# A Mamba and attention kernel on one core: three exps ahead, three work banks, and an input added by a transfer

## The chip, the core and the metric

The kernel runs on one core of one Trainium2 chip. The core has engines that run side by side, each through its own queue of instructions in order: PE (TensorE, matrix products into PSUM), DVE (VectorE), ACT (ScalarE), POOL (GpSimd) and SP (SyncE, which here only issues DMA transfers). The metric is the device time of one execution in microseconds (us), the median of the runs. Time before: 8270.61 us, median of 3 runs (8264.9 to 8275.63).

## The reference, cut to what matters

The input x has 4 images of 512 channels and 64 x 64 positions, in float32. Two layers are added to it, each on its group norm:

```python
# layer 0: group norm, layer norm over the channels, then 4 chunks of 128 channels through one Mamba
x = x + mamba_block(_gn(x))
# inside, for each chunk: in_proj, a causal convolution of 4 taps, silu, then for each position
h = exp(dt * A) * h + (dt * xc) * B        # 256 inner channels x 16 states
y = (h * C).sum(over states)
# y + xc * D, times silu(z), out_proj, plus skip * chunk; layer norm; a projection 512 -> 512
# layer 1: linear attention with 8 heads on the group norm of the result
x = x + attention(_gn(x))                  # q, k relu; kq = k^T q over all positions; out_proj
```

The recurrence over the 4096 positions of an image is what takes most of the time. The group norm of layer 1 needs the statistics of the whole image after layer 0, so an image's attention starts when its last tile has left layer 0.

## The kernel before, in words

**Steps and slots.** A tile is 512 positions of one image. A step is one tile and one chunk of 128 channels: 4 images x 8 tiles x 4 chunks = 128 steps, numbered n, with c the chunk. A step has 16 slots (SLOTS), and each slot s is one function call, `slot`. In it DVE runs two scans of 128 x 512 (L602: h = dA * h + bx along the positions), which need an exp dA from ACT (L576, `decay`) and a product bx from POOL (L584, `drive`, issued two slots ahead). `decay` writes dA into PSUM, in a pool of LEAD banks; the exp for scan k + LEAD is put in ACT's queue behind scan k, and can start when scan k has read its bank. Then DVE multiplies the states of one slot by C (L625, `product`), mostly between the two scans of the next slot; in slots 3 and 11 the slot's own product comes at its end as well, and slots 4 and 12 have none. C's rows come from PE, which spreads them to 128 partitions in the one bank c_all (`c_row`), once for two slots: it can be filled when the second product has read it and must be full for the next one. The last quarter of the positions is multiplied by POOL (L613). `fold_states` lets PE sum the states into y.

**The order of the work.** Inside `tc.manual_schedule()` the instructions stand as the Python code issues them. At the end of each slot `after` issues the rest: first what is due, then fixed items by slot number (softplus of the next step's dt in slot 2, with two table loads; the copy `with_skip` in slot 5; silu in slot 10), then pieces of the background work. That work is written as generators in the queues `ahead` (the next tile's norms), `late` (`projected`: the second layer norm, the projection 512 to 512 and the sum with x) and `rest` (the attention of the image before). A budget of matmuls (`credit`) and the number of PSUM banks held (`limit[0]`, asked for by `room`) say how much of it is let in.

**Banks and results.** PSUM has eight banks: y 1, c_all 1, dA LEAD = 2, and four work banks (`ps_w`) that all other matmul groups share. A group's result is taken from its bank by ACT (or DVE). `later(2, what)` issues that copy two slots after the matmuls, so that the engine that takes it does not stand waiting for PE.

**The sum with x** (`projected`, L413 to L443): the tile of x is loaded again by SP into a buffer xr (`load_x`), of which there are three, shared by tag with the attention's tiles. PE adds it to the projection in the bank with four small matmuls at once against a 32 x 32 identity, `fold`; ACT takes the sum and its bias into xr (L421); one slot later DVE takes the group norm's statistics of that quarter (L423, `bn_stats`); SP stores the tile (L442).

**After the slots** the last image's projection and attention run alone, bounded by PE.

Of the kernel before, what the change touches and what calls it, by code (L numbers as in the profile page):

```python
# [14 lines left out]
P = 128  # L15
T = 512
# [8 lines left out]
def kernel(  # L25
# [40 lines left out]
    wk = ctx.enter_context(tc.tile_pool(name="wk", bufs=2))  # L66
    LEAD = 2

# [3 lines left out]
    ps_d = ctx.enter_context(tc.tile_pool(name="ps_d", bufs=LEAD, space=bass.MemoryType.PSUM))  # L72
    ps_w = ctx.enter_context(tc.tile_pool(name="ps_w", bufs=4, space=bass.MemoryType.PSUM))

# [49 lines left out]
    def no_tile(spare=0):  # L124
        return now[0] is not None and held_x[0] + spare >= TILES

    def load_now(src, name):
        held_x[0] += 1
        xt = wk.tile([P, NC, T], F32, tag="x", name=name, bufs=TILES)
        nc.sync.dma_start(xt, src)  # L130
        return xt
# [163 lines left out]
    def stats_end(stats, name):  # L295

        mv = small.tile([P, NC, 2], F32, tag="mv", name=f"mv_{name}")
        for c in range(NC):
            nc.vector.bn_aggr(mv[:, c, :], stats[:, c, :, :].rearrange("p t s -> p (t s)"))
        cm = small.tile([P, NC], F32, tag="cm", name=f"cm_{name}")  # L300
        nc.vector.tensor_copy(cm, mv[:, :, 0])
        pm = work_bank(f"pm_{name}")
        mm(pm[:, 0:NC], grp, cm, start=True, stop=True)
        gm = small.tile([P, NC], F32, tag="gm", name=f"gm_{name}")
        nc.vector.tensor_copy(gm, pm[:, 0:NC])
        dev = small.tile([P, NC], F32, tag="dev", name=f"dev_{name}")
        nc.vector.tensor_tensor(dev, cm, gm, ALU.subtract)
        nc.vector.tensor_tensor(dev, dev, dev, ALU.mult)
        nc.vector.tensor_tensor(dev, dev, mv[:, :, 1], ALU.add)
        pv = work_bank(f"pv_{name}")  # L310
        mm(pv[:, 0:NC], grp, dev, start=True, stop=True)
        gr = small.tile([P, NC], F32, tag="gr", name=f"gr_{name}", bufs=4)
        nc.vector.tensor_scalar(gr, pv[:, 0:NC], 1e-5, None, ALU.add)
        free(2)
# [21 lines left out]
    def layer_norm(v, name, gained):  # L336


        def means(parts, what, when):
            yield from room()  # L340
            sums = work_bank(f"{what}_sums_{name}")
            for c in range(NC):
                mm(
                    sums[c * LANE : (c + 1) * LANE, :], ones, parts[c],
                    start=True, stop=True, abreast=NC,
                )
            got = wk.tile([P, T], F32, tag="sq", name=f"{what}_got_{name}", bufs=4)

            def take():
                nc.scalar.copy(got, sums)  # L350
                free()

            copied = later(2, take)
            yield
            yield from until(copied)
            yield when
            yield from room(when)
            bank = work_bank(f"{what}_{name}")
            mm(bank, mean.to_broadcast([P, P]), got, start=True, stop=True)
            return bank  # L360
# [21 lines left out]

        rooted = later(2, root)
        yield
# [28 lines left out]
    def projected(ym, stats, x1, b, t):  # L413

        nm = f"{b}_{t}"
        yield from layer_norm(ym, f"b_{nm}", False)
        xt = yield from load_x(b, t, "r")
        taken = []

        def take(o, pp):  # L420
            nc.scalar.activation(xt[:, o, :], pp, AF.Identity, bias=pb[:, o : o + 1])  # L421
            free()
            later(1, lambda: nc.vector.bn_stats(stats[:, o, t, :], xt[:, o, :]))  # L423

        for o in range(NC):
            yield from room()
            pp = work_bank(f"pp_{nm}_{o}")
            for c in range(NC):
                mm(
                    pp, w_pr[:, c, o * P : (o + 1) * P], ym[:, c, :],  # L430
                    start=(c == 0), stop=False,
                )
                if c == 1:
                    yield "more"
            for k in range(P // BLK):
                r = slice(k * BLK, (k + 1) * BLK)
                mm(pp[r, :], fold[r, :], xt[r, o, :], abreast=P // BLK, start=False, stop=True)
            taken.append(later(2, lambda o=o, pp=pp: take(o, pp)))
            yield
        yield from until(*taken)  # L440
        yield from pause(1)
        nc.sync.dma_start(x1, xt)  # L442
        later(2, free_x)  # L443


    def inputs(f, xn, c, nm):
# [14 lines left out]
        for e in range(NH):  # L461
            pc[e] = work_bank(f"pc_{nm}_{e}", 0)
            taps(e, range(NTAP // 2))
            yield
            taps(e, range(NTAP // 2, NTAP))
            later(2, lambda e=e: take(e))
            yield
        for e in range(NH):
# [5 lines left out]

            later(2, lambda e=e, pz=pz: nc.scalar.copy(xz[:, 1, e, :], pz))
            yield
# [197 lines left out]
    def attention(b, x1s, stats):  # L674
# [35 lines left out]
        def sums(v):  # L710
# [5 lines left out]
            for p in range(NC):  # L716
                for i in range(P // HEAD):
# [4 lines left out]
                    )  # L722
            return later(2, lambda: add(pk, v == 0))

        fetch(0, "a")
        yield
        norm = stats_end(stats, f"b{b}")
        yield
        for v in range(NT * SUB):
# [5 lines left out]
            for j in range(2):  # L735
# [14 lines left out]
                qk[i] = both[:, 1 + i % 3, :]  # L750
                ready[i] = later(2, lambda i=i, pq=pq: relu(i, pq))
                if u:
# [34 lines left out]
        for p in range(NC):  # L787
            yield from room()
            pm = work_bank(f"pm2_{b}_{p}")
            mm(pm, kqn[:, p, :], m2[:, p, :], start=True, stop=True)  # L790
            taken.append(later(2, lambda p=p, pm=pm: take2(p, pm)))
            yield
# [11 lines left out]
        for m in range(NC):  # L804
            yield from room()
            pm = work_bank(f"pm3_{b}_{m}")
            for p in range(NC):
# [4 lines left out]
                if p == 1:  # L812
                    yield "more"
            taken.append(later(2, lambda m=m, pm=pm: take3(m, pm)))
            yield
# [9 lines left out]
        for o in range(NC):  # L825
# [7 lines left out]
            for m in range(NC):  # L833
# [3 lines left out]
                )  # L837
            taken.append(later(2, lambda o=o, pm=pm: offset(o, pm)))
            yield
# [14 lines left out]
        for t in range(NT):  # L854
            x1 = yield from fetched(t, "b")
            for o in range(NC):
                yield from room()
                pp = work_bank(f"pr_{b}_{t}_{o}")
                for m in range(NC):
# [4 lines left out]
                    if m == 1:  # L864
                        yield "more"
                later(2, lambda t=t, o=o, pp=pp: store(t, o, pp))
                fetch(t + 1, "b")
# [21 lines left out]
    def input_norm(b):  # L889
        stats = stats_tile(f"st0_{b}")  # L890
        yield from stats0(stats, b)
        norms[b] = stats_end(stats, f"a{b}")
        yield
# [71 lines left out]
    with tc.manual_schedule():  # L965
        credit, seen, mix, held[0], held_x[0] = 0.0, work["mm"], iter(()), 0, 0
        for n, (b, t, c) in enumerate(steps):
# [10 lines left out]
            for s in range(SLOTS):  # L978
                def after():
# [17 lines left out]
                    if s == 2 and nxt is not None:  # L997
                        nc.scalar.preload_act_table_set("softplus")
                        time_steps(nxt, names[n + 1])
                        nc.scalar.preload_act_table_set("natural_log_exp_and_others")  # L1000
                    if s == 5 and before is not None:
                        pb_, pt_, pc_ = steps[n - 1]
# [28 lines left out]

                    limit[0] = 3 if 9 <= s < 13 else 2
                    credit = min(credit + 3.5 - (work["mm"] - seen), 2.6)
# [76 lines left out]
```

## Time and profile before

| | before |
|---|---|
| median of 3 runs | 8270.61 us |
| the profiled execution's own time | 8270.61 us |
| its span | 8268.9 us |
| busy: PE | 6698.2 us (81%) |
| busy: DVE | 7187.9 us (87%) |
| busy: ACT | 5366.3 us (65%) |
| busy: POOL | 6856.1 us (83%) |
| first scan, last scan begin | 122.5 us, 7805.7 us |

A row of a group has the line, the engine and the operation, what it writes and reads, how often; then the busy time of all, the mean of one in ns, and the idle time of the engine just before them with what ended it. A wait has who waited, for whom, the total in us, the number and the longest. A row of the timeline has its start, its length, and in brackets the idle time before it.

### The profile page before, as it was taken

To read this page: it belongs to the slowest core of one execution; us is meant where nothing else is said; L and a number is where in the kernel's file an instruction comes from. 1 tells how busy PE (TensorE), PEld (TensorE's weight loads), DVE (VectorE), ACT (ScalarE), POOL (GpSimd) and SP (SyncE) were. 2 spreads that over 40 slices of the span, in tenths; PEclk is the share of its full clock that TensorE was granted. 3 is DMA by queue.
4 is the path that set the end of the run, shared out by engine and by line. 5 is a ranking of instruction groups with operands and counts; after the bars stand their busy time and mean duration, and the time that the engine had idled before them with its cause. 6 is when DMAs were issued, how large, how long until landed. Compare 5 with 4: busy or idle time off the path is not lost. (4 is left out here: it accounts for less than half of the span.)

```text
span 8268.9 us, 89639 instructions
## 1 busy us (share of the span) xinstructions
PE 6698.2 (81%) x23450; PEld 2248.1 (27%) x23520; DVE 7187.9 (87%) x6890; ACT 5366.3 (65%) x7841; POOL 6856.1 (83%) x4565
## 2 busy tenths in 40 slices
PE   5677777767788888888788888888788888888699
PEld 1122222112222222322222222232223223233244
DVE  5999999999999999988999999988889999998700
ACT  4666666666666776666677766667667666666421
POOL 4999899999888888888888988888889888888600
PEclk8788888778899989999899999899889999989799
DMA  5666665666666666666666666566666655666412
GB/s 159 165 162 160 146 152 144 155 148 159 164 162 151 155 161 151 161 177 169 165 153 161 164 160 160 149 161 179 161 154 157 156 144 148 152 175 180 120 39 87
DMA packets 829317, 1266.32 MB, mean 153 GB/s; under 512 B 183920, under 2 KB 317568, under 8 KB 816512
## 3 DMA queue, kind: packets, MB, share of 16 engines
q1 hardware_dynamic: 821632, 1255.87, 60.3%
q10 hardware_dynamic: 7168, 4.71, 0.2%
q8 instruction: 184, 3.01, 0.2%
q14 instruction: 333, 2.73, 0.1%
HBM read 1053.28 MB, written 206.57 MB: 152 GB/s over the span
## 5 line engine op out<-in xcount | busy, mean ns | idle before, releaser
L584 POOL TENSOR_TENSOR bx<-d_all,b_all 128x1024 f32<-128x1024 f32 x2048 | 4793.8, 2360 | 98.7 <-DVE h L602 82.1
L602 DVE TENSOR_TENSOR_SCAN h<-dA,st,bx 128x512 f32<-128x512 f32 x3584 | 4432.6, 1269 | 236.4 <-ACT dA L576 141.8
L576 ACT ACTIVATE dA<-d_all,a_t 128x512 f32<-128x512 f32 x4096 | 2803.6, 689 | 2227.3 <-DVE h L602 2202.4
L625 DVE TENSOR_TENSOR h<-h,c_all 128x768 f32<-128x768 f32 x2048 | 1909.2, 932 | 256.0 <-PE c_all L120 246.1
L613 POOL TENSOR_TENSOR h<-h,c_sb 128x512 f32<-128x512 f32 x1024 | 1298.2, 1268 | 110.4 <-DMA c_sb<-c_rows 18.3
L120 PE MATMUL y<-h,fold 128*32 128x512 f32 x8192 | 1278.2, 700 | 122.7 <-POOL h L613 118.7
L120 PE MATMUL c_all<-parts,sel 128*128 128x384 bf16 x1024 | 374.2, 365 | 1097.2 <-DVE h L625 1094.7
L120 PE MATMUL pq<-w_qk,xa 128*128 128x512 f32 x2048 | 1039.8, 640 | 10.7 <-issue 5.1
L120 PE MATMUL pc<-xn,w_cv 128*128 128x512 f32 x2048 | 1015.5, 626 | 39.9 <-ACT res L850 15.6
L612 POOL COPY st<-h 128x4 f32<-128x4 f32 x1024 | 192.7, 188 | 631.1 <-DVE h L602 583.5
L602 DVE TENSOR_TENSOR_SCAN h<-dA,bx 128x512 f32<-128x512 f32 x512 | 602.7, 1209 | 93.3 <-ACT dA L576 84.4
L120 PEld LDWEIGHTS <-sel 128*128 128x128 bf16 x1280 | 127.7, 100 | 1864.8 <-DVE h L625 1632.3
L120 PEld LDWEIGHTS pc<-xn,w_cv 128*128 128x128 f32 x2048 | 377.8, 197 | 698.9 <-issue 564.0
L120 PEld LDWEIGHTS pq<-w_qk,xa 128*128 128x128 f32 x2048 | 411.4, 205 | 496.2 <-issue 472.9
L120 PE MATMUL pr<-xb,m 128*128 128x512 f32 x1024 | 514.5, 641 | 7.9 <-ACT parts L531 5.9
L120 PE MATMUL pp<-xn,w_pr 128*128 128x512 f32 x1024 | 516.3, 630 | 3.8 <-DVE xn L387 3.8
L120 PE MATMUL pt<-dt,w_dt 32*128 32x512 f32 x512 | 270.7, 885 | 108.1 <-ACT parts L531 55.0
L120 PEld LDWEIGHTS y<-h,fold 128*32 128x32 f32 x8192 | 171.0, 114 | 665.9 <-issue 343.9
L120 PE MATMUL y<-xz,dg 128*128 128x512 f32 x512 | 344.6, 763 | 0.0
L649 POOL TENSOR_TENSOR xz<-xz 128x512 f32<-128x512 f32 x256 | 325.2, 1270 | 2.7 <-ACT xz L646 2.7
L494 POOL TENSOR_TENSOR dt<-dt,xz 128x1024 f32<-128x1024 f32 x128 | 302.6, 2364 | 20.7 <-DMA c_rows<-dt 20.7
L120 PE MATMUL pd<-xz,w_xp 128*128 128x512 f32 x512 | 293.1, 702 | 7.8 <-ACT xz L919 7.8
(156 smaller groups left out, 6141.9 us busy)
## 6 DMA issues: line engine op xcount, KB each, us to landing
d_all<-d_rows SPq DMA_DIRECT2D x2048, 256.0 KB, 6.6
b_all<-b_rows SPq DMA_DIRECT2D x4096, 64.0 KB, 2.2
d_rows<-dt SPq DMA_DIRECT2D x256, 512.0 KB, 2.8
c_sb<-c_rows SPq DMA_DIRECT2D x4096, 16.0 KB, 1.8
xs<-in_x_dram SPq DMA_DIRECT2D x32, 1024.0 KB, 6.8
xn<-in_x_dram SPq DMA_DIRECT2D x32, 1024.0 KB, 6.1
xr<-in_x_dram SPq DMA_DIRECT2D x32, 1024.0 KB, 6.1
x<-xr SPq DMA_DIRECT2D x32, 1024.0 KB, 4.3
```

The source lines that it names most:

```text
L120: nc.tensor.matmul(out_, lhsT, rhs, **how)
L494: nc.gpsimd.tensor_tensor(f["both"][:, 1], f["both"][:, 0], f["xz"][:, 0], ALU.mult)
L576: nc.scalar.activation(dAs[k], fs[n]["d_all", e][:, 0, j, :], AF.Exp, scale=a_t[:, e, j, q : q + 1])
L584: nc.gpsimd.tensor_tensor(bxs[g], fs[n]["d_all", e][:, 1, jj * 2 : jj * 2 + 2, :], bc(b_all[g // JJ], 2), ALU.mult)
L602: nc.vector.tensor_tensor_scan(h[:, j, :], dAs.pop(2 * g + i), bxs[g][:, i, :], 0.0 if t == 0 else st[:, c, e, q, j : j + 1], ALU.mult, AL ...
L612: nc.gpsimd.tensor_copy(st[:, c, e, q, :], h[:, :, T - 1])
L613: nc.gpsimd.tensor_tensor(h[:, :, CUT:], h[:, :, CUT:], bc(c_sb.pop(g // JJ), NJ), ALU.mult)
L625: nc.vector.tensor_tensor(own, own, bc(c_all[g // JJ], 2), ALU.mult)
L649: nc.gpsimd.tensor_tensor(f["xz"][:, 1, e, :], f["xz"][:, 1, e, :], f["xz"][:, 0, e, :], ALU.mult)
```

## The change

LEAD becomes 3, which gives dA three banks and puts the exp for scan k + 3 behind scan k; the work banks become three. Nearly every `later(2, ...)` that takes a result becomes `later(1, ...)`; `with_skip` goes from slot 5 to slot 4. The two tiny groups of `stats_end` share a bank, and `stats_end` becomes a generator that asks for room. The limit of banks held becomes 1 in slots 15 and 0 to 3 and 2 elsewhere (before: 3 in slots 9 to 12, 2 elsewhere). In `projected` the load of x and the four fold matmuls go. ACT writes the projection and its bias into a fresh buffer; then a transfer issued by POOL adds x to it in SBUF (`accum_op=ALU.add`); the statistics are taken four slots later, two quarters a slot, and then the tile is stored.

```diff
-    LEAD = 2
+    LEAD = 3
...
-    ps_w = ctx.enter_context(tc.tile_pool(name="ps_w", bufs=4, space=bass.MemoryType.PSUM))
+    ps_w = ctx.enter_context(tc.tile_pool(name="ps_w", bufs=3, space=bass.MemoryType.PSUM))
...
+    def new_tile(name):
+        held_x[0] += 1
+        return wk.tile([P, NC, T], F32, tag="x", name=name, bufs=TILES)
+
     def load_now(src, name):
-        held_x[0] += 1
-        xt = wk.tile([P, NC, T], F32, tag="x", name=name, bufs=TILES)
+        xt = new_tile(name)
         nc.sync.dma_start(xt, src)
...
+        yield from room()
         pm = work_bank(f"pm_{name}")
...
-        pv = work_bank(f"pv_{name}")
-        mm(pv[:, 0:NC], grp, dev, start=True, stop=True)
+        pv = pm[:, NC : 2 * NC]
+        mm(pv, grp, dev, start=True, stop=True)
...
-            copied = later(2, take)
+            copied = later(1, take)
...
-        rooted = later(2, root)
+        rooted = later(1, root)
...
         yield from layer_norm(ym, f"b_{nm}", False)
-        xt = yield from load_x(b, t, "r")
+        while no_tile():
+            yield "wait"
+        xt = new_tile(f"xr_{nm}")
         taken = []
 
         def take(o, pp):
             nc.scalar.activation(xt[:, o, :], pp, AF.Identity, bias=pb[:, o : o + 1])
             free()
-            later(1, lambda: nc.vector.bn_stats(stats[:, o, t, :], xt[:, o, :]))
...
-                    start=(c == 0), stop=False,
+                    start=(c == 0), stop=(c == NC - 1),
                 )
                 if c == 1:
                     yield "more"
-            for k in range(P // BLK):
-                r = slice(k * BLK, (k + 1) * BLK)
-                mm(pp[r, :], fold[r, :], xt[r, o, :], abreast=P // BLK, start=False, stop=True)
-            taken.append(later(2, lambda o=o, pp=pp: take(o, pp)))
+            taken.append(later(1, lambda o=o, pp=pp: take(o, pp)))
             yield
         yield from until(*taken)
-        yield from pause(1)
+
+        nc.gpsimd.dma_start(xt, cols(x, b)[:, :, t * T : (t + 1) * T], accum_op=ALU.add)
+        yield from pause(4)
+        for o in range(NC):
+            nc.vector.bn_stats(stats[:, o, t, :], xt[:, o, :])
+            if o % 2:
+                yield
         nc.sync.dma_start(x1, xt)
         later(2, free_x)
...
-            later(2, lambda e=e: take(e))
+            later(1, lambda e=e: take(e))
...
-            later(2, lambda e=e, pz=pz: nc.scalar.copy(xz[:, 1, e, :], pz))
+            later(1, lambda e=e, pz=pz: nc.scalar.copy(xz[:, 1, e, :], pz))
...
-                ready[i] = later(2, lambda i=i, pq=pq: relu(i, pq))
+                ready[i] = later(1, lambda i=i, pq=pq: relu(i, pq))
...
-                    if s == 5 and before is not None:
+                    if s == 4 and before is not None:
...
-                    limit[0] = 3 if 9 <= s < 13 else 2
+                    limit[0] = 1 if s in (SLOTS - 1, 0, 1, 2, 3) else 2
```

The attention's other results (`add`, `take2`, `take3`, `offset`, `store`) change from `later(2, ...)` to `later(1, ...)` in the same way, and the callers of `stats_end` take its result with `yield from`.

More of the change, by code (lines that the diff above doesn't have):

```diff
@@ L309, in stats_end @@
         nc.vector.tensor_tensor(dev, dev, mv[:, :, 1], ALU.add)
-        pv = work_bank(f"pv_{name}")
-        mm(pv[:, 0:NC], grp, dev, start=True, stop=True)
+        pv = pm[:, NC : 2 * NC]
+        mm(pv, grp, dev, start=True, stop=True)
         gr = small.tile([P, NC], F32, tag="gr", name=f"gr_{name}", bufs=4)
-        nc.vector.tensor_scalar(gr, pv[:, 0:NC], 1e-5, None, ALU.add)
-        free(2)
+        nc.vector.tensor_scalar(gr, pv, 1e-5, None, ALU.add)
+        free()
         nc.gpsimd.tensor_tensor(gr, gr, mhalf, ALU.pow)
@@ L722, in sums @@
                     )
-            return later(2, lambda: add(pk, v == 0))
+            return later(1, lambda: add(pk, v == 0))
         fetch(0, "a")
         yield
-        norm = stats_end(stats, f"b{b}")
+        norm = yield from stats_end(stats, f"b{b}")
         yield
@@ L790, in attention @@
             mm(pm, kqn[:, p, :], m2[:, p, :], start=True, stop=True)
-            taken.append(later(2, lambda p=p, pm=pm: take2(p, pm)))
+            taken.append(later(1, lambda p=p, pm=pm: take2(p, pm)))
             yield
@@ L813, in attention @@
                     yield "more"
-            taken.append(later(2, lambda m=m, pm=pm: take3(m, pm)))
+            taken.append(later(1, lambda m=m, pm=pm: take3(m, pm)))
             yield
@@ L837, in attention @@
                 )
-            taken.append(later(2, lambda o=o, pm=pm: offset(o, pm)))
+            taken.append(later(1, lambda o=o, pm=pm: offset(o, pm)))
             yield
@@ L865, in attention @@
                         yield "more"
-                later(2, lambda t=t, o=o, pp=pp: store(t, o, pp))
+                later(1, lambda t=t, o=o, pp=pp: store(t, o, pp))
                 fetch(t + 1, "b")
@@ L891, in input_norm @@
         yield from stats0(stats, b)
-        norms[b] = stats_end(stats, f"a{b}")
+        norms[b] = yield from stats_end(stats, f"a{b}")
         yield
```

## The prediction

> **What bounds the kernel now.** I read the busy shares first, then the same shares by stretch, then VectorE's waits, and last the timeline around the longest of them.
>
> ```profile
> L602 DVE TENSOR_TENSOR_SCAN h<-dA,st,bx 128x512 f32<-128x512 f32 x3584 | 4432.6, 1269 | 236.4 <-ACT dA L576 141.8
> L584 POOL TENSOR_TENSOR bx<-d_all,b_all 128x1024 f32<-128x1024 f32 x2048 | 4793.8, 2360 | 98.7 <-DVE h L602 82.1
> ...
> 150.00:7810.00 7660.00, 6191.50 (x21765) 2020.27 (x21817) 7096.15 (x6708) 5217.00 (x7621) 6818.43 (x4531) 0.88 0.64 159
> 7810.00:8269.00 459.00, 435.32 (x1520) 199.11 (x1532) 28.68 (x75) 97.03 (x150) 2.27 (x2) 0.94 0.16 58
> ```
>
> The columns of the stretches are PE, PE's weight loads, DVE, ACT, POOL. From 150 to 7810 us the slots run: 2048 of them, two scans and one product each. There DVE is busy 7096 of 7660 us. It sets the pace, and 564 us of idle DVE is all that this change can win, since it takes no work from DVE. POOL has 842 us idle there, PE 1468, ACT 2443. The last 459 us belong to PE.
>
> VectorE's own waits in that stretch:
>
> ```profile
> DVE h L625 <- PE c_all L120: 246.1, 114, 11.2
> DVE h L602 <- ACT dA L576: 177.1, 171, 6.4
> DVE h L602 <- issue: 55.0, 37, 3.2
> DVE h L602 <- POOL h L613: 25.1, 25, 2.4
> ```
>
> The product waits for the C rows that TensorE puts into the single bank c_all; the scan waits for ScalarE's exp. I added these idle times up by the slot s of their step of 16. c_all: 86 us in slot 3, 92 in slot 7, 58 in slot 15, 9 in slot 9. Exps and "issue": 73 us in slot 4, 93 in slot 12, 36 in slot 3. So few places carry the idle time. Two of them, PE rows with the DVE row that waits:
>
> ```profile
> 5792.23 1.88 PE L120 MATMUL pp<-xn,w_pr 128*128 128x512 f32 x4
> 5800.99 1.93 PE L120 MATMUL pp<-xr,fold 32*32 32x512 f32 x8 [6.88 <-DMA xr<-in_x_dram]
> 5806.30 0.33 PE L120 MATMUL c_all<-parts,sel 128*128 128x384 bf16 x1
> 5806.66 0.96 DVE L625 TENSOR_TENSOR h<-h,c_all 128x768 f32<-128x768 f32 x1 [9.42 <-PE c_all L120]
> ...
> 2330.94 1.64 PE L120 MATMUL pt<-dt,w_dt 32*128 32x512 f32 x2 [2.61 <-ACT parts L531]
> 2332.51 3.78 PE L120 MATMUL pq<-w_qk,xa 128*128 128x512 f32 x4
> 2336.08 0.53 PE L120 MATMUL c_all<-parts,sel 128*128 128x384 bf16 x1
> 2336.65 0.95 DVE L625 TENSOR_TENSOR h<-h,c_all 128x768 f32<-128x768 f32 x1 [3.79 <-PE c_all L120]
> ```
>
> First (slot 15): the fold that adds the input cannot start until the input has landed, and c_all stands behind it in PE's queue. Second (slot 3): pt waits for a bank or its data from ACT, then two pq matmuls go ahead of c_all. An exp that is late in slot 4, after ACT's two table loads and two softpluses, in DVE's timeline:
>
> ```profile
> 1987.06 3.45 DVE L602 TENSOR_TENSOR_SCAN h<-dA,bx 128x512 f32<-128x512 f32 x3 [2.40 <-ACT dA L576]
> ```
>
> POOL's longest wait in the slots, and a row of the chain that ended last, after them:
>
> ```profile
> POOL st L612 <- DVE h L602: 582.2, 625, 7.8
> ...
> 8152.52 112.75 PE pr L120 x256
> ```
>
> POOL mostly waits for DVE, not the reverse. The second row gives a matmul's price: 128 matmuls (two records each) in 112.75 us, 0.88 us.
>
> **What the Trainium skill says.** "DMA: Bandwidth & Descriptors", section "SWDGE vs HWDGE vs iDMA": a transfer that accumulates can only be issued from GpSimd, whose cores compute its descriptors in software. Its section "Latency and other measured facts" puts about 1 us before the first byte, and "The descriptor swizzle" counts 288 descriptors for 1 MiB in 128 rows. The trace of before has no such transfer. "SBUF — State Buffer", section "Who interferes with whom": a VectorE instruction with one SBUF input, outside the 2-port modes, does not contend with GpSimd. Scan and product each read one operand from PSUM, and the scan's 1187 to 1286 ns over 4096 rows agree. "Perfetto Trace Analysis", section "Matmuls": groups should rotate through banks so that evacuation overlaps the next group; with 4 banks PE's waits for evictions are small (pt 103 us, the others under 70).
>
> **The change part by part.**
>
> *Exps three ahead.* The same 4096 exps, each free to run one scan (1.27 us) earlier. Taking 1.25 us off each of the 171 waits leaves 60 of 177 us: -117. "Issue" sits in the same slots 4 and 12; the same cut leaves 19 of 55; I take -25. The cover is POOL: bx for slot 6 is ready only 0.6 us (median) before its scan, but POOL waits for DVE in slot 3, so it follows DVE's clock and this margin stays.
>
> *The fold and the load.* 1024 fold records (140.2 us of PE) and 32 loads on SP's queue go. PE is not the bound, so only slot 15 counts: 16 of its 18 waits are in the third step of a tile, where pp stands. I take -50 of 58.
>
> *Where PE work is let in* (one bank allowed in slots 15 and 0 to 3, two elsewhere, instead of two, and three in 9 to 12). Read off PE's order in both built programs at 0.88 us a matmul, the work between the filling of c_all for products 0 and 1 and that for 2 and 3 (product 2 waits in slot 3) falls from 3.3 to 2.1 us in second steps of a tile and from 3.8 to 2.1 in third ones, which carry 77 of the 86 us: -70. The work between the fillings for products 4, 5 and 6, 7 (product 6 waits in slot 7) rises from 8.5 to 9.6 us (second steps) and from 9.7 to 10.5 (third). Some 10.4 us are available there (slots 4, 5, 6 and one scan: 2.5+3.3+3.3+1.3). At 32 steps each this is +35 and +26 if all of it shows, less what the earlier start saves (the example's slot-3 wait started this stretch 1.3 us late): I take +20, ends 0 and +61. So c_all goes from 246 to about 146.
>
> *Three banks, results one slot earlier.* By the built orders, the cases in which a bank is taken again in the very slot in which ACT empties it rise from 307 to 430, most for pt after pd and pz after pc. PE then waits until the end of that slot's scans plus about 1.4 us; c_all cannot be filled sooner either, as the product comes half a slot later: nothing, unless ACT is late. ACT itself may now stand waiting for PE, with exps behind it. I took every eviction of before that moves (with_skip's copy in slot 5 too), set it one slot earlier, let it wait for its matmul's end, added the eviction and one exp, and compared with the start of the scan that needs that exp at a lead of three: 50 cases are late, by 46 us in all. +46, ends 0 and +150, as bursts add up and PE itself moves.
>
> *The adding transfer.* 31 in the slots, issued by POOL in slots 13 and 15 of a third step, behind ACT's last write of xr. Queued behind it: the bx of the slot after next, and st. bx has 2.4 to 3.6 us to spare in slots 0 to 2, so an issue under about 2.5 us is covered; each us above costs 31 us. The source has 512 runs of 2 KB, 1056 descriptors by the page's way of counting against its 288, so 1 to 3.7 us as an estimate from the page's 1 us: I take 2, which is nothing; ends 0 and +37. VectorE's bn_stats wait for the landing: four slots are 13.6 us or more, less some 2 until POOL issues. A plain load of this size lands in 3.8 to 10.8 us (median 5.9); doubled for the read of the destination, 11.8 in the median. I take +10, ends 0 and +80. bn_stats itself only moves (128 x 0.67 us).
>
> *Ends.* After the last scan both programs have the same matmuls but the fold. There bn_stats waits for the transfer: landing 6 to 12 us, three bn_stats no longer under the matmuls (2 us), less four folds (1.06 us each): +4 to +10, taken +8. Three banks in the prologue: +2. In the last loop ACT's one result buffer, not the banks, is nearly as slow as PE: nothing.
>
> Sum: -117 -25 -50 -70 +20 +46 +10 +8 +2 = -176 us. The profiled execution took 8270.6 us for a span of 8268.9, which is also the median. 8270.6 - 176 = 8095 us, 2.1% less.
>
> **The rivals.**
> (1) *The freed time turns into other waits.* ACT's waits for PE and PE's for banks come at their upper end (+150 instead of +46) and slot 7 at +61: 8095 + 104 + 41 = 8240. For it: the work ahead of slot 7's c_all is already at its limit. Against it: the PE rows that make ACT wait are the ones that DVE waits for anyway, so these waits overlap. Around 8200 with half of it.
> (2) *Slower: the adding transfer.* Place: POOL's issue in slots 13 and 15. POOL is the second busiest engine and in order. Its slack is 2.5 us, so the gain (176 us, 5.7 us a tile) is eaten when an issue takes 8.2 us; at 11 us the kernel takes 8095 + 31 x 8.5 = 8359. For it: the price is unseen here, and 11 us would be only 10 ns for each of 1056 descriptors made in software. Against it: POOL sits idle 225 and 116 us in just these slots, and the page's price.
> (3) *Better: the waits vanish whole.* Exps and issue leave 30 us rather than 90, and slot 7 falls with the earlier start: 8095 - 60 - 50 = 7985. For it: ACT is only 65% busy and refills a third buffer soon.
>
> **How the numbers follow.** The sum 0.48 (8040 to 8150), rival 1 0.20 (8150 to 8254), rival 3 0.13, rival 2 or more bank stalls than thought 0.15 (8287 and up), within 0.2% 0.04. This kernel's measurement cannot tell less than about 0.2% from no change. Faster: 0.48+0.20+0.13 = 0.81. 7990 to 8290 leaves out about half of rival 3 and nearly all of rival 2, 0.2 in all.
>
> **What would show it.** Right: DVE busy in the slots unchanged near 7096 us; waits for dA under 110 us; c_all near 146 us and now nearly all in slot 7; no PE wait for xr; POOL's wait for DVE below 582 us, since DVE wastes less. Wrong: a DVE wait of bn_stats for the transfer over 100 us, bx waits over 50 us (POOL's issue is dear), or dA waits still at 177 us with ACT waiting for pq, pp and pc (results taken too early).

## The result, and the profile after

The changed kernel takes 8214.98 us, median of 4 runs (8214.01 to 8225.66), against 8273.12 us for the kernel before (4 runs, 8264.9 to 8278.96): ratio 0.9933, interval 0.9916 to 0.9951. It is faster by 0.7%. The forecast was 8095 us, 2.1% faster; a third of the gain came, and the time lies between that forecast and rival 1 in full (8240).

First the busy times by stretch, as before (length, PE, PE's weight loads, DVE, ACT, POOL, granted clock, DMA share, GB/s), of the kernel after:

```profile
150.00:7754.00 7604.00, 6163.21 (x20824) 2030.12 (x20824) 7094.28 (x6707) 5196.51 (x7619) 6850.59 (x4562) 0.87 0.64 160
7754.00:8213.00 459.00, 425.00 (x1504) 194.85 (x1500) 27.77 (x75) 96.92 (x150) 3.63 (x3) 0.95 0.18 60
```

DVE's work in the slots is the same (7094 against 7096 us), and the part after the slots is as long as before. So nearly all of the 56 us by which the slots got shorter is idle time of DVE: 564 us before, 510 after. DVE's waits in the slots of the kernel after:

```profile
DVE h L610 <- ACT dA L584: 206.6, 144, 5.6
DVE h L633 <- PE c_all L120: 142.5, 102, 3.7
DVE kq L715 <- PE pk L120: 78.2, 53, 5.7
DVE h L610 <- POOL bx L592: 25.1, 25, 2.9
DVE ob L830 <- PE pob L120: 18.8, 9, 3.0
```

The wait for c_all fell from 246 to 143 us. The wait for exps hardly fell: dA and "issue" together were 232 us and are 207, all of it dA. And two rows are new: DVE stands for pk and pob, results of the attention that DVE itself takes from PSUM (97 us together, 4 before). The wait for bx grew too; in the kernel before the row was

```profile
DVE h L602 <- POOL bx L584: 3.6, 3, 1.5
```

ScalarE, which makes the exps, now waits in the slots for things for which it hardly waited before. ACT's own waits after:

```profile
ACT kq L708 <- PE pq L120: 144.3, 82, 6.1
ACT xn L668 <- PE po L120: 105.3, 71, 7.0
ACT xz L654 <- PE y L120: 85.0, 97, 4.9
ACT xn L329 <- DMA xn<-in_x_dram: 80.5, 29, 9.1
ACT xr L427 <- PE pp L120: 61.4, 68, 2.1
```

and of the kernel before:

```profile
ACT xz L646 <- PE y L120: 54.3, 83, 2.8
ACT xr L421 <- PE pp L120: 41.9, 18, 8.0
ACT xn L325 <- DMA xn<-in_x_dram: 37.2, 23, 6.2
ACT kq L700 <- PE pq L120: 19.6, 11, 2.6
```

What this does to an exp is seen where the prediction looked too, in slot 4 of a tile's first step. ACT's timeline of the kernel after, with the DVE row that waits at its end:

```profile
6555.87 1.52 ACT L329 ACTIVATE xn<-xn,off_a,gr_a 128x512 f32<-128x512 f32 x2 [3.76 <-DMA xn<-in_x_dram]
6557.30 1.28 ACT L584 ACTIVATE dA<-d_all,a_t 128x512 f32<-128x512 f32 x2
6558.61 0.60 ACT L708 ACTIVATE kq<-pq 128x512 f32<-128x512 f32 x1
6559.22 1.28 ACT L1006 ACT_TABLE_LOAD   x1
6560.52 1.27 ACT L495 ACTIVATE dt<-pt,dtb 128x512 f32<-128x512 f32 x2
6561.80 1.28 ACT L1008 ACT_TABLE_LOAD   x1
6563.10 1.52 ACT L329 ACTIVATE xn<-xn,off_a,gr_a 128x512 f32<-128x512 f32 x2
6564.52 1.90 ACT L584 ACTIVATE dA<-d_all,a_t 128x512 f32<-128x512 f32 x3
...
6565.23 1.28 DVE L610 TENSOR_TENSOR_SCAN h<-dA,st,bx 128x512 f32<-128x512 f32 x1 [3.76 <-ACT dA L584]
```

ACT stands 3.76 us for the load of xn. Two exps follow at 6557.30, and then some 5.9 us of other ACT work (a relu, the softplus between two table loads, half a group norm) before the next exp. Three exps made in good time would nearly span this block (three scans and two products take DVE 3 x 1.27 + 2 x 0.93 = 5.7 us); the wait ahead of it has used them up, and DVE waits 3.76 us, just as long as ACT did. Added up by slot, the waits for exps and "issue" in the first steps' slots 3 and 4 are 98 us, against 96 before: there nothing was gained.

DVE's new wait, with the PE and ACT rows around it:

```profile
4829.28 1.06 PE L120 MATMUL y<-h,fold 128*32 128x512 f32 x8 [3.68 <-POOL h L621]
4830.27 1.78 PE L120 MATMUL pz<-xn,w_z 128*128 128x512 f32 x2
4831.98 1.12 PE L120 MATMUL pk<-kq 128*64 128x64 f32 x16
...
4830.41 0.58 ACT L654 COPY xz<-y 128x512 f32<-128x512 f32 x1 [3.84 <-PE y L120]
...
4833.15 0.42 DVE L715 TENSOR_TENSOR kq<-pk,kq 128x256 f32<-128x256 f32 x1 [5.10 <-PE pk L120]
```

PE waits for POOL's last quarter of the product, and pz and pk are queued behind y. The copy of y on ACT, whose place the change leaves alone, and the add of pk on DVE, now issued one slot after its matmuls, stand still with PE. A slot takes 3.7 us in the mean (7604 us for 2048), so a second slot in between would cover most of such a wait.

### The profile page after: what moved, and what is told of

It reads as the page before. It is cut to its first block, busy times and chain, and to the rows that moved or that the text cites. A ratio compares the mean times of both kernels' runs of the same rounds, so it can differ in the third digit from the quotient of the medians.

```text
span 8212.9 us, 87683 instructions
## 1 busy us (share of the span) xinstructions
PE 6659.6 (81%) x22496; PEld 2253.4 (27%) x22496; DVE 7185.7 (87%) x6890; ACT 5346.7 (65%) x7841; POOL 6889.7 (84%) x4597
## 4 chain that ended last, share of the span: by engine, by line
PE 27%; DMA 17%; DVE 17%; POOL 13%; issue 9%; ACT 9%; SPq 8%; POOLq 0%; DVEq 0%; ACTq 0%
DVE h L610 11%; DMA d_all<-d_rows 9%; POOL bx L592 8%; PE pq L120 5%; PE y L120 5%; DVE h L633 5%; SPq L559 5%; PE pc L120 4%; ACT dA L584 4%; DMA b_all<-b_rows 3%; PE pr L120 3%; SPq L513 3%; POOL h L621 2%; PE po L120 2%; PE pp L120 2%
## 5 line engine op out<-in xcount | busy, mean ns | idle before, releaser
L584 ACT ACTIVATE dA<-d_all,a_t 128x512 f32<-128x512 f32 x4096 | 2765.5, 688 | 1629.8 <-DVE h L610 1579.3
L120 PE MATMUL y<-h,fold 128*32 128x512 f32 x8192 | 1327.3, 725 | 273.2 <-POOL h L621 269.1
L120 PE MATMUL pq<-w_qk,xa 128*128 128x512 f32 x2048 | 1005.6, 625 | 1.6 <-ACT xa L329 1.6
L120 PE MATMUL pp<-xn,w_pr 128*128 128x512 f32 x1024 | 492.5, 613 | 3.8 <-DVE xn L391 3.8
L120 PE MATMUL pt<-dt,w_dt 32*128 32x512 f32 x512 | 378.2, 943 | 141.2 <-ACT parts L539 126.8
L708 ACT ACTIVATE kq<-pq 128x512 f32<-128x512 f32 x256 | 151.7, 593 | 339.9 <-PE pq L120 338.7
L120 PE MATMUL y<-xz,dg 128*128 128x512 f32 x512 | 364.8, 804 | 0.0
```

The costliest lines, as they stand in the source:

```text
L120: nc.tensor.matmul(out_, lhsT, rhs, **how)
L584: nc.scalar.activation(dAs[k], fs[n]["d_all", e][:, 0, j, :], AF.Exp, scale=a_t[:, e, j, q : q + 1])
L708: nc.scalar.activation(qk[i], pq, AF.Relu)
```

## The experiments

All times below are medians of 4 runs or more; the kernel before took 8274.6 to 8279.1 us beside them. A difference between two changed kernels is one of medians; worked out from their ratios to the kernel before it comes out up to 9 us away. The table has DVE's idle time between the first and the last scan, and its waits from 150 us on, from one profiled execution each.

| kernel | us | idle of DVE | exps and "issue" | c_all | pk and pob |
|---|---|---|---|---|---|
| before | 8273 | 564 | 232 | 246 | 4 |
| before + adding transfer | 8269 | 559 | 240 | 216 | 4 |
| after, two exps, four work banks, old limit | 8437 | 703 | 479 | 50 | 50 |
| after, two exps | 8450 | 719 | 442 | 27 | 77 |
| after | 8215 | 509 | 207 | 143 | 97 |
| after, pk and offset taken at two slots | 8181 | 473 | 191 | 209 | 2 |
| after, group norm of xn one slot later | 8183 | 478 | 153 | 153 | 104 |
| after, three ACT results taken at two slots | 8201 | 495 | 146 | 224 | 73 |
| after, copy with the skip in slot 5 | 8227 | 511 | 191 | 162 | 99 |
| after, less work on PE | 8165 | 462 | 180 | 105 | 112 |
| pk and xn together | 8137 | 425 | 131 | 212 | 2 |
| pk, xn and three ACT results | 8179 | 468 | 76 | 302 | 2 |
| after without the transfer | 8204 | 510 | 149 | 160 | 70 |
| pk and xn without the transfer | 8169 | 465 | 123 | 220 | 2 |

**What each part is worth.** The theory formed from the two traces: results taken one slot after their matmuls make ACT and DVE, each working through its queue in order, stand for PE, and the third exp is spent on that. Its main rival: PE's lateness only moves from one wait to the next, wherever results are taken. The expectations name their theories by letters, each in its own text. First the third exp alone is taken away.

```diff
-    LEAD = 3
+    LEAD = 2
```

> The changed kernel with two exps ahead instead of three (one PSUM bank stays unused); all else as changed. Theory A (the third exp does pay, but pays for ACT's new waits for PE): dA waits rise from 207 to 330 us or more, the time to about 8340, above the kernel before. Rival B (the third exp is worth nothing, since what delays exps is not the lead): dA waits within 30 us of 207, the time within 30 us of 8215.

Measured: 8449.5 us, ratio to before 1.0206 (1.0189 to 1.0223). This is theory A, and more of it than expected. DVE's waits in the slots:

```profile
DVE h L610 <- ACT dA L584: 381.6, 271, 6.3
DVE h L633 <- PE c_all L120: 27.4, 28, 3.5
```

The third exp is worth 8449.5 - 8215.0 = 234 us in this kernel, 92 more than the 142 that the prediction took for it. One row of ACT in this run will matter below:

```profile
ACT xn L329 <- DMA xn<-in_x_dram: 38.9, 24, 6.1
```

With two exps ACT waits 39 us for the load of xn, nearly as little as before (37), and with three 80 us. Then the work banks and the limit go back to those of before as well, so that against the kernel before what remains is the early results (with the skip's copy and the shared bank of the statistics) and the transfer.

```diff
-    LEAD = 3
+    LEAD = 2
-    ps_w = ctx.enter_context(tc.tile_pool(name="ps_w", bufs=3, space=bass.MemoryType.PSUM))
+    ps_w = ctx.enter_context(tc.tile_pool(name="ps_w", bufs=4, space=bass.MemoryType.PSUM))
-                    limit[0] = 1 if s in (SLOTS - 1, 0, 1, 2, 3) else 2
+                    limit[0] = 3 if 9 <= s < 13 else 2
```

> The changed kernel with two exps, four work banks and the former limit of banks: the kernel before with the results taken one slot earlier and with the transfer, which alone changed nothing. Theory A (early taking is the price): dA waits about 330 to 380 us as with two exps and three banks, the time 8400 or more. Rival D (three banks and the tighter limit are the price): dA near 180 to 230 us, the time within 40 us of 8270.

Measured: 8437.47 us, ratio 1.0191 (1.0176 to 1.0206).

```profile
DVE h L610 <- ACT dA L584: 424.2, 292, 6.9
DVE h L633 <- PE c_all L120: 49.6, 36, 5.0
```

This is theory A. With two exps and four banks the early results cost about 165 us (the ratios 1.0191 here and 0.9993 for the transfer alone, below, are 0.0198 apart, and 0.0198 x 8273 = 164, if the transfer is worth the same in both): the waits for exps and "issue" double, and ACT's waits for PE, added up, go from 136 to 485 us. No run takes all results late with three exps, so their price in the kernel after is known only for the parts taken back below. Three banks and the limit add some 12 us more (1.0206 against 1.0191), which the two intervals don't tell from nothing. Note c_all: with the old limit and four banks it is at 50 us already. A DVE that waits for exps comes later to the product, which would leave PE time to fill c_all. The waits are no separate accounts.

The transfer by itself, put into the kernel before:

```diff
-            for k in range(P // BLK):
-                r = slice(k * BLK, (k + 1) * BLK)
-                mm(pp[r, :], fold[r, :], xt[r, o, :], abreast=P // BLK, start=False, stop=True)
...
+        nc.gpsimd.dma_start(xt, cols(x, b)[:, :, t * T : (t + 1) * T], accum_op=ALU.add)
+        yield from pause(4)
```

> The kernel before with one part of the change alone: x added by POOL's transfer instead of by fold matmuls, statistics four slots later. Theory A (PE's wait for x goes and nothing else changes): the c_all waits of slot 15 fall from 58 us to under 15, the time falls by 40 to 60 us to about 8220. Rival C (the transfer is dear for POOL): 31 issues of 1.3 us plus POOL's wait for ACT's last write, 55 us in the changed kernel, push bx back: bx waits over 40 us, the time within 20 us of 8270 or above.

Measured: 8268.52 us (20 runs), ratio 0.9993 (0.9986 to 1.0000): no change. That is rival C's time, but not its reason.

```profile
DVE h L609 <- ACT dA L583: 232.1, 205, 5.5
DVE h L632 <- PE c_all L120: 216.3, 122, 5.6
DVE st L446 <- DMA xr<-in_x_dram: 20.2, 9, 3.4
```

In slot 15 c_all falls from 58 to 16 us as the prediction said, and the sum does not move: c_all in slot 3 rises from 86 to 105, the exps' waits of slot 12 from 62 to 95, and bn_stats waits 20 us for the landing. Rival C's sign, bx waits over 40 us, did not appear (11 us).

The same question was put to the kernel after, by undoing the transfer there.

```diff
-        while no_tile():
-            yield "wait"
-        xt = new_tile(f"xr_{nm}")
+        xt = yield from load_x(b, t, "r")
...
+            later(1, lambda: nc.vector.bn_stats(stats[:, o, t, :], xt[:, o, :]))
...
+            for k in range(P // BLK):
+                r = slice(k * BLK, (k + 1) * BLK)
+                mm(pp[r, :], fold[r, :], xt[r, o, :], abreast=P // BLK, start=False, stop=True)
...
-        nc.gpsimd.dma_start(xt, cols(x, b)[:, :, t * T : (t + 1) * T], accum_op=ALU.add)
-        yield from pause(4)
```

> The kernel after with the fold matmuls, SP's load and the bn_stats one slot after each quarter put back in place of the adding transfer; three exps, three work banks and early results stay. Theory A (the transfer's price and gain cancel, as they did when it was put alone into the kernel before): within 20 us of the kernel after, 8195 to 8235 us. Theory B (with one bank allowed in slot 15 the folds in front of c_all count, as the prediction's term of 50 us said): 8245 to 8275 us, with c_all in slot 15 at 60 us or more instead of 27.

Measured: 8204.32 us, ratio 0.9911 (0.9895 to 0.9928), which isn't told apart from the kernel after. c_all in slot 15 is 49 us, 22 more than in after but below the 60 of theory B; price and gain cancel again. A row appears that neither theory had:

```profile
DVE h L629 <- PE c_all L120: 159.5, 103, 5.9
DVE st L427 <- ACT xr L425: 75.5, 25, 5.0
DVE h L606 <- POOL bx L588: 8.6, 13, 1.9
```

bn_stats, one slot behind a take that is itself one slot behind its matmuls, makes DVE wait for ACT. The four slots that the transfer's version leaves before bn_stats do away with that. No run keeps the fold and moves bn_stats back, so the transfer itself and the later statistics are not told apart. The wait for bx falls from 25 to 9 us.

**The waits at their places.** DVE's two takings go back to two slots after their matmuls; all else stays.

```diff
-            return later(1, lambda: add(pk, v == 0))
+            return later(2, lambda: add(pk, v == 0))
...
-            taken.append(later(1, lambda o=o, pm=pm: offset(o, pm)))
+            taken.append(later(2, lambda o=o, pm=pm: offset(o, pm)))
```

> The changed kernel with only DVE's own takings from the work banks (the sum of pk into kq, and the offset) back at two slots after their matmuls. Theory A (taken one slot later, results are asked for before PE has them, and the asking engine stands): DVE's wait for pk in the slots falls from 78 us to under 10 and that for pob from 19 to under 8, c_all and dA stay near 143 and 207 us, and the time falls by 60 to 85 us, to about 8140. Rival B (the freed time only turns into other waits, PE being the limit there): pk's wait goes, but c_all and dA take it over, and the time stays within 20 us of 8215.

Measured: 8181.07 us, ratio 0.9887 (0.9872 to 0.9901), 34 us less than after: more than rival B allows, about half of what theory A asks.

```profile
DVE h L633 <- PE c_all L120: 208.9, 149, 7.4
DVE h L610 <- ACT dA L584: 190.6, 143, 5.8
```

The 97 us of pk and pob are gone, and 66 of c_all come in their place: 46 of them in slot 15 (27 to 73), right behind the slots 13 and 14 in which pk had been waited for. About a third is kept.

Next ACT's wait for the load of xn, of which the timeline above shows one case. The load and the group norm that needs it are one slot apart; this puts another slot between them.

```diff
         nc.sync.dma_start(body, cols(x, b)[:, :, t * T : (t + 1) * T])
         yield "free"
+        yield from pause(1)
```

> The changed kernel with one slot more between the load of the next tile and its group norm on ACT. Theory A2 (in slot 4 of a tile's first step the exps are late because ACT stands for that load, 80 us in slot 2, whatever the lead): ACT's wait for xn falls below 10 us, the dA waits of slots 3 and 4 from 100 us to under 30, the time by 50 to 80 us to about 8150. Rival (they are late for the table loads and the softplus of slot 2): dA in slot 4 stays within 20 us of 82, the time within 15 us of 8215.

Measured: 8182.87 us, ratio 0.9884 (0.9869 to 0.9899), 32 us less than after: again between the two theories.

```profile
DVE h L634 <- PE c_all L120: 153.4, 106, 3.9
DVE h L611 <- ACT dA L585: 153.3, 139, 4.4
```

The wait for exps falls by 53 us, of which slot 4 gives 31 (82 to 51) and slot 3 gives 18; ACT's wait for this load falls from 80 to 3 us. Of the 53 us less of waiting, 32 are kept. Then relu, store and the projection's take, the ACT results for which ACT waited long, go back to two slots.

```diff
-                ready[i] = later(1, lambda i=i, pq=pq: relu(i, pq))
+                ready[i] = later(2, lambda i=i, pq=pq: relu(i, pq))
...
-            taken.append(later(1, lambda o=o, pp=pp: take(o, pp)))
+            taken.append(later(2, lambda o=o, pp=pp: take(o, pp)))
```

(and `store` likewise.)

> The changed kernel with three of ACT's takings (q and k's relu, the attention's store, the projection's result) back at two slots after their matmuls; banks, lead and the rest as changed. Theory A (ACT stands waiting for PE with exps behind it): ACT's waits for pq, pr and pp in the slots fall from 257 us to under 60, dA waits from 207 to about 140, the time by 50 to 70 us, to about 8155. Rival D (three banks are too few to hold results longer): PE waits for banks instead, c_all waits rise by as much as dA waits fall, and the time stays within 20 us of 8215 or goes up.

Measured: 8200.7 us, ratio 0.9912 (0.9897 to 0.9926), not told apart from the kernel after, as rival D has it. The wait for exps falls by 61 us to 146, so these results do hold exps up; but c_all rises by 82 to 224, of which slot 7 has 126 (78 in the kernel after). A result held one slot longer holds one of three banks longer, which would explain it. All of ScalarE's results at two slots with three banks, and three banks with the old limit, were not measured.

The copy `with_skip`, by which ACT takes po (the output projection with its skip), back in slot 5:

```diff
-                    if s == 4 and before is not None:
+                    if s == 5 and before is not None:
```

> The changed kernel with the copy of with_skip back in slot 5, one slot after its matmuls have been asked for more time. Theory A (ACT's place in line matters: it stands 105 us for po with the exps of slots 6 and 7 behind it): ACT's wait for po falls below 20 us, the dA waits of slot 6 from 42 us to under 15, the time by 20 to 40 us to about 8185. Rival B (PE's lateness only moves): dA waits stay within 20 us of 207, c_all rises, the time within 15 us of 8215.

Measured: 8226.81 us, ratio 0.9937 (0.9922 to 0.9952): not told apart from after, and no gain: rival B, against theory A. The exps' wait in slot 6 fell from 42 to 25 us and c_all's in slot 7 rose from 78 to 94.

Is PE simply too late everywhere? This kernel leaves out part of the computation: taps 1 and 2 of the convolution are not done on PE, while the budget counts them, so that the other work stays where it is.

```diff
             for k in ks:
+                if k in (1, 2):
+                    continue
...
+            work["mm"] += 2.0
```

> The changed kernel with taps 1 and 2 of the convolution left out of PE's work (512 of its matmuls, some 500 us of PE; their place in the budget is kept, so all other work stands where it stood). Rival B (PE's lateness is behind c_all, pk and the exps' waits alike): c_all from 143 to under 50 us, ACT's waits for PE from some 600 to under 350 us, dA from 207 to under 130, the time down by 120 us or more, to 8090 or less. Theory A alone (only the places at which results are asked for): c_all falls, but dA and pk stay near 207 and 78 us, the time stays above 8130.

Measured: 8165.28 us, ratio 0.9864 (0.9848 to 0.9881), 50 us less than after, for 286 us less work on PE in the slots (some 500 us were planned; the granted clock was 0.858 here and 0.874 in after). By its time this is theory A.

```profile
DVE kq L718 <- PE pk L120: 94.4, 42, 6.1
```

c_all in slot 7 falls from 78 to 23 us. The waits for pk rise (78 to 94), slot 4 keeps its 81 us of exps, and ACT's waits for PE stay at 588 us (592). So c_all in slot 7 goes with PE's load; the waits for pk and the exps of slot 4 do not. For pk the run before with its later taking shows what they go with, and for slot 4 the later norm of xn does for 31 of the 82 us.

**Together.** The two edits that gained most, in one kernel:

```diff
+        yield from pause(1)
...
-            return later(1, lambda: add(pk, v == 0))
+            return later(2, lambda: add(pk, v == 0))
...
-            taken.append(later(1, lambda o=o, pm=pm: offset(o, pm)))
+            taken.append(later(2, lambda o=o, pm=pm: offset(o, pm)))
```

> The kernel after with the two edits that gained most, together: VectorE takes pk and the parts' offsets two slots after their products, as the kernel before did, and the group norm of xn stands one slot later behind its load. Alone they gave 34 and 32 us. Theory A (two different waits, VectorE standing for pk and ScalarE standing for xn's load with exps behind it): the gains add, 8140 to 8160 us, no wait of VectorE for pk, dA about 150 us or less, c_all about 210. Theory B (time freed at one place is lost again at the next, since TensorE's convolution has to follow in the same tile): 8170 to 8190 us, not better than either alone, c_all 230 or more.

Measured: 8136.97 us (8135.75 to 8144.18), ratio 0.9829 (0.9813 to 0.9846): better than both kernels, by 1.7% than before and about 1% than after.

```profile
DVE h L634 <- PE c_all L120: 212.1, 146, 8.4
DVE h L611 <- ACT dA L585: 131.0, 131, 3.0
```

Alone they gave 34 and 32 us, together 78: the gains add, as theory A says, and the 12 us on top are within the intervals. No exp is waited for longer than 3.0 us. ACT's waits for PE, added up, are larger than in the kernel after (688 us against 592), and yet exps are late by less. The sum of ACT's waits does not tell what they cost. The timeline above suggests that it counts whether a block of other work comes right behind; that was not tested apart from the load of xn.

With relu, store and take at two slots as well:

```diff
-                ready[i] = later(1, lambda i=i, pq=pq: relu(i, pq))
+                ready[i] = later(2, lambda i=i, pq=pq: relu(i, pq))
...
-            taken.append(later(1, lambda o=o, pp=pp: take(o, pp)))
+            taken.append(later(2, lambda o=o, pp=pp: take(o, pp)))
...
-            later(1, lambda t=t, o=o, pp=pp: store(t, o, pp))
+            later(2, lambda t=t, o=o, pp=pp: store(t, o, pp))
```

> The former with ScalarE's relu, store and projection results taken two slots after their products as well, so that results are taken as early as in the kernel after only where the buffers leave no choice. Alone this gave 14 us, and moved 82 us from dA to c_all. Theory A: 8125 to 8150 us, dA 120 or less. Theory B: 8180 to 8200 us, with dA down and c_all at 270 or more, since the work banks then come free a slot later and the convolution starts later.

Measured: 8179.29 us, ratio 0.9882 (0.9867 to 0.9897): 42 us worse, close to theory B.

```profile
DVE h L634 <- PE c_all L120: 302.2, 175, 7.0
DVE h L611 <- ACT dA L585: 76.0, 87, 3.4
```

The exps' wait falls as expected and c_all takes more than all of it, 169 us in slot 7 alone. Here the gain is lost at the next place. With three banks, taking these three results early is worth 42 us in this kernel, while in the kernel after nothing was told apart (14 us the other way).

Last, the best version with the transfer undone by the edit shown above:

> The same put back in the kernel that combines the later taking of pk with the later group norm of xn (8137 us with the transfer). Theory A: 8120 to 8155 us. Theory B: 8165 to 8190 us, with c_all in slot 15 at 100 us or more instead of 75.

Measured: 8168.78 us, ratio 0.9871 (0.9857 to 0.9886). The transfer with its later statistics is worth 32 us in this kernel. The time is that of theory B, its reason is not: c_all in slot 15 fell (75 to 49 us) instead of rising, and a wait of bn_stats for ACT appears, as above:

```profile
DVE st L428 <- ACT xr L426: 50.9, 16, 5.9
```

## Why the prediction was wrong, step by step

The direction and the range were right, the size was not: -58 us instead of -176. Five kernels of the table form a chain in which each step puts in one more part of the change: before, before with the transfer, then with the early results (two exps, four banks), then with three banks and the new limit (two exps), and after. From their ratios to the kernel before, times 8273:

| part, in this order | forecast | measured |
|---|---|---|
| transfer in place of fold and load, landing and tail (-50 + 10 + 8) | -32 | -6 |
| results one slot earlier | +46 | +164 |
| three banks and the limit (-70 + 20 + 2) | -48 | +12 |
| third exp (-117 - 25) | -142 | -226 |

What falls to a part depends on the order: with two exps DVE waits so much for exps that c_all has only 50 us left to lose, and a third exp put into the kernel before was not measured.

- **Three banks, results one slot earlier (+46, ends 0 and +150).** This is the step that failed: a slot less before taking a result was priced at 46 us and took 164, though measured with two exps where the forecast was for three. The prediction let each of ACT's evictions wait for its matmul at the times of the kernel before. In the run, ACT's waits for PE grew from 136 to 485 us and exps were waited for twice as long. This is rival 1's mechanism, which the prediction held back with "these waits overlap".
- **The same step left out DVE and POOL, that is, put them at nothing.** It counted only ACT's evictions. `add` and `offset` are DVE instructions in that list, and DVE is the engine that sets the pace: 97 us of new waits in the trace, of which the run without them gives back 34 us of time. For DVE a taking that has to wait isn't covered by any lead. POOL's case is under the transfer's issue.
- **Exps three ahead (-117 and -25).** The cut of 1.25 us off each wait assumed that ACT uses its freedom to come earlier. In slots 3 and 4 of the first steps that cut would have left 47 of 96 us, and 98 were measured. There ACT came earlier to the load of xn and stood for it: 39 us with two exps, 80 with three. The run with one slot more takes 49 us of the exps' waits in slots 3 and 4 away and 32 us of time. Elsewhere the third exp paid more than forecast, against the late exps that the early results make.
- **How far this explains the time.** Later takings on DVE and the later norm of xn together give 78 of the 118 us that are missing. The other 40 are not placed, and what the two edits would give in the kernel before was not measured.
- **The fold and the load (-50), landing (+10), tail (+8).** The place was right (58 to 16 us in slot 15 when done alone) but it was no gain: no change in time alone, none told apart in the kernel after, 32 us in the best version, where the place of bn_stats has a share that no run separates. Put in alone, the wait removed in slot 15 came back in slots 3 and 12.
- **The limit (-70) and slot 7 (+20).** c_all came to 143 us where 146 was forecast, and this is partly luck. With pk taken later it is 209; with late exps it is 50 under the old limit. The limit's own share stays open, since no run changes it alone.
- **The adding transfer's issue on POOL (0, ends 0 and +37).** The price of the issue was right, its place was not. The Trainium skill's page "DMA: Bandwidth & Descriptors" puts about 1 us before the first byte of such a transfer ("Latency and other measured facts"), from which the prediction's estimate of 1 to 3.7 us was made. What the trace has is the time of the issuing instruction; in the view of tile xr of the kernel after (shortest, median and longest in ns; then us to landing):

```profile
L444 POOL DMA_DIRECT2D xr<-in_x_dram x32: 1299/1302/1495, 508.0 to 7793.1; - x32
...
DMA to landing us min/median/max: 3.8/8.8/10.6
```

1.30 us is under the 2.5 us that bx had to spare. But POOL first stands for ACT's last write of xr, a wait that the prediction named in order and put at nothing:

```profile
POOL xr L444 <- ACT xr L427: 54.9, 31, 3.5
```

With 1.8 us of it each time and 1.3 for the issue, bx comes late: of DVE's 25 us of waiting for bx, 21 are in slots 15 and 0. With the transfer alone, where ACT's results are still taken at two slots, POOL waits 8 us. So this is the early taking again, on a third engine. PE's wait for POOL ahead of y grows too: 119 us before, 269 after, 179 in the kernel after without the transfer. bn_stats did not wait for a landing in the slots. Rival 2, in which the issue takes 8 us and more, is out, and so is rival 3.

- **Of the signs named ahead**, DVE's busy time, no PE wait for xr, c_all near 146 and POOL's wait for DVE (382 us, below 582) came true. c_all was not nearly all in slot 7 (78 of 143), and exps were not under 110. The sign for "wrong" that did appear was "dA waits still at 177 us with ACT waiting for pq, pp and pc": they are at 207, with 144 and 61 us for pq and pp.
- **Two readings of the prediction don't come out.** Half of rival 1 is 72 us on top of 8095, which makes 8168 and not "around 8200". And POOL's idle time in slot 13 of the kernel before is 173 us by the order of its own instructions, not 225. Neither changes the argument.
- The Trainium skill's statement on VectorE and GpSimd, in "SBUF — State Buffer", section "Who interferes with whom", that a VectorE instruction with one SBUF input does not contend with GpSimd outside the 2-port modes, agrees with this trace too: the scans took 1190 to 1296 ns after, 1187 to 1286 before, with POOL busy for 90% of the slots.

Why ACT's wait for the load of xn grew from 37 to 80 us shows in the run with two exps, which differs from the kernel after in nothing else. Over the 25 loads in each trace whose landing is recorded, ACT is ready for the load 5.2 us after its issue in the mean with two exps and 3.8 us with three, about one scan (1.27 us) sooner; the load lands after 6.5 and 6.6 us. What stays open is the remaining 40 us, and what each of ACT's early results costs with three exps.

## What to carry to other kernels

A result taken earlier from PSUM frees a bank and puts an in-order engine behind PE: list every engine that takes results, or issues something behind one that does, the bound one first. A wait ahead of a block of other work should be counted at full length and not at its mean; here this rests on the load of xn alone. A lead of more buffers is spent once; before booking its whole gain, look at which other part of the change draws on the same lead, and whether the engine that comes earlier only meets another wait earlier. When waits trade with each other (here c_all, exps and pk), value an edit by the bound engine's whole idle time, and not by the row that it removes.

## What the runs showed of the hardware

An accumulating transfer of 1 MiB into SBUF cost its issuing engine, POOL, 1.30 us in the median, about as much as one of its own 128 x 512 multiplications (1.27 us). It landed after 8.8 us in the median, against 5.9 us for the plain load that it replaced: less than the doubling that the prediction had assumed (11.8).
